# Steps of the cross-attention chain that go on in every cell, and a norm that waits for the queries alone

## The chip, the cores and the metric

The kernel runs on one core of one Trainium2 chip. The metric is the device time of one execution in microseconds; the times of before are those of three runs. The profile is that of one more execution of the same program, with a time of its own.

## What is computed

Two layers work on the same stream of tokens `x`, 2 sequences of 1024 tokens with 256 features, in float32. A context of 64 tokens for each sequence, and a mask over it, come beside it. Both layers have 16 heads of 16 features.

```python
# layer 0
x = x + mha(ln(x), ln(x))                  # self attention, 1024 x 1024 scores per head
x = x + mha(ln_q(x), ln_kv(context))       # cross attention, 1024 x 64 scores per head
h = ln(x); top 2 of 8 experts by h @ router
x = x + sum(gate * (gelu(h @ fc1[e]) @ fc2[e]))
# layer 1
x = x + proj(attention(qkv(ln0(x))))       # self attention
attn = softmax(q(ln1(x)) @ k(context).T * SCALE + (1 - mask) * -10000)
x = x + proj(attn @ v(context))            # cross attention, masked
x = x + fc2(gelu(fc1(ln2(x))))
```

## The kernel before

Tokens lie in tiles of 128; a unit is 512 tokens (four tiles), so that there are four units, two for each sequence. PE's results go to eight PSUM banks that are handed out by `bank()` and given back to the list `free`. PE, DVE, ACT and SP execute in the order in which the program was written down[...].

**The cells of self attention.** `self_attention` (L527) walks through cells (the loop at L960): 64 for each sequence, so 128 cells and two more to finish. A cell is one head, 512 queries and 128 keys in both of two kinds of scores. In each cell stand four score matmuls "b" (L817), whose exponentials ACT takes (L823), and, `LEAD` = 10 cells ahead, four score matmuls "a" (L806), whose maxima DVE takes (L813). In cells 0 to 117 there is something left to look ahead to (`has_a`); `maxima[0]` says so to the rest of the program. Every second cell has the product of exponentials and values (L868) of two cells, whose results ACT copies (L880) and POOL adds up (L881). At the end of a head its maxima are turned into the subtrahend of its queries (`largest`, L714 and L716). The sums of a finished group of heads travel over DRAM (SP: L482, L483, L487, `turns` L499, `by_s` L503), and POOL multiplies by them (L509).

**Everything else is a stream of steps.** All other work is cut into tasks, Python generators that issue some instructions and yield. `Stream` (L132) decides, when the program is built, after which cell a step is issued. A yield above zero is the declared cost of the step, in us of PE; a yield of zero or below declares no cost and asks for a pause, to the next cell or, below zero, for that many us, counted in cells of `CELL` = 2.9 us. `owed` is what the stream may still spend: each cell adds `pace(cell)`, at least the layer's `RATE` (2.5 us in layer 0, 1.1 in layer 1), and it is capped at 3.0 before that. While `owed` exceeds 0.6, `Stream.step` takes a step of the ready task with the earliest last cell, then the highest rank. Steps without cost are also taken only there. In an even cell with `owed` below 2.5 the loop goes straight on to the next cell. What must be there by then is forced with `Stream.until`: `need_heads` (L703) forces the projections that an even head needs in the cell whose look-ahead reaches it. When the loop is over, `Stream.rest` (L179) issues what is left by rank and readiness.

**Tasks.** Keys and queries (`keys` L656, `queries` L665) project a pair of groups of heads and then spread it with eight small DMAs on SP (`spread_head`, L650 to L652, into `KS` and `QS`), in two steps of four without cost. The self attention's output projection of a unit (`project`, L788, its task `go`) has two halves of 2.0 each. Then the chain of cross attention follows for the units in turn (`cross_tasks`, L1077):

- `norm` (mark "cnorm"): the layer norm of four tiles, its turning by PE (L370) and copying by ACT (L377); two steps of 1.0.
- `weigh` (L1104, mark "weighed"): two projections of queries (L1114, 1.72 each), then scores, softmax, turning and products for two groups. If `maxima[0]` holds as it starts, it takes the whole form: scores are copied by ACT (L1159), the mask is added by POOL (L1178), maxima and sums are DVE's (L1168, L1191), the subtraction and division POOL's or DVE's (L1169, L1193), the exponentials ACT's (L1185), and then come the turning (L1201), its copy (L1206) and the product. Otherwise, in layer 1, PE adds the mask with matmuls (L1139), ACT takes exponentials from the turned scores (L1208), and PE makes the sums (L1240, `undivided`) and spreads the reciprocals (L1255, `division`).
- `share` (L1317, mark "cross"): the output projection of cross attention, two halves of 2.0.

In layer 0 `dispatch_task` (L1351) of a unit comes next (norm, router, places of the tokens with their experts; `found` and `rows` follow it) and then the slots of the experts. In layer 1 `forward_norm` (L1844, mark "ready", four roots on POOL: L332 to L335) and `forward_task` (L1852, L1861 and L1873) follow, with 29.8 for each unit.

The order of the chain before: the norm of unit n waits for the mark ("weighed", n - 1), and the whole `weigh` of unit n for its norm and for ("cross", n - 1).

Of the kernel before, what the change touches and what calls it, by code (L numbers as in the profile page):

```python
# [121 lines left out]
class Task:  # L122

    def __init__(self, steps, cost, first=-99, last=None, mark=None, after=(), rank=0):
        self.steps, self.left, self.first = steps, cost, first
        self.soft, self.last = last is None, 9999 if last is None else last
        self.mark, self.after, self.rank = mark, after, rank


class Stream:  # L132
# [20 lines left out]
    def step(self, cell):  # L153
        while True:
            able = [t for t in self.tasks if t.first <= cell and self.made.issuperset(t.after)]
            if not able:
                return None
            cost = self.advance(min(able, key=lambda t: (t.last, -t.rank)), cell)
            if cost and cost > 0.0:
                return cost  # L160

    def pace(self, cell):

# [39 lines left out]
def two_blocks(  # L203
# [228 lines left out]
    def project_task(src, w, first, t0, n):  # L432

        i, p = bank()
        p = p.rearrange("p (c d) -> p c d", d=D)
        for c in range(n):
            for k in range(2):
                nc.tensor.matmul(  # L438
                    p[:, c, :],
                    lhsT=src[:, k, (t0 + c) * P : (t0 + c + 1) * P],  # L440
                    rhs=w[:, W_O + k * D : W_O + (k + 1) * D],
                    start=(k == 0),
                    stop=(k == 1),
                )
        xb = x_sb[:, first : first + n, :]
        nc.vector.tensor_tensor(xb, xb, p[:, :n, :], ALU.add)
        free.append(i)
        yield 2.0
# [78 lines left out]
    def self_attention(layer, tail, heads, arrive, extra, when_ready, beside=None):  # L527
# [5 lines left out]
        w = weights[att]  # L533
# [32 lines left out]
        now = [-99]  # L566
# [221 lines left out]
        def project(b, qh, after=()):  # L788
            def go():
                for t0 in range(0, 4, 2):  # L790
                    yield from project_task(ot[b, qh], w, b * TB + 4 * qh + t0, t0, 2)
                when_ready(b, qh, stream, now[0])

            stream.add(go(), 4.0, last=now[0] + 4, rank=60, after=after)

        def score(kind, cell, j):
            h, n = divmod(cell, 8)
# [162 lines left out]
        for cell in range(ncell + 2):  # L960
            now[0] = cell
            ahead = cell + LEAD
            if ahead < ncell and ahead % 16 == 0:
                need_heads(ahead // 8)
            has_a, has_b = ahead < ncell, cell < ncell
            maxima[0] = has_a
            a = [("a", ahead, j) for j in (2, 3, 0, 1)] if has_a else []
            s = [("b", cell, j) for j in range(4)] if has_b else []
            if has_a:
                slot(s[:2] + a[:2])  # L970
                slot(s[2:] + a[2:])
            elif has_b:
                slot(s)
            if ahead % 8 == 7 and has_a:
                h = ahead // 8
                collect(h)
                stream.add(largest(h), 0.75, first=cell + 1, last=cell + 2, mark=("QB", h))
            if (cell + 1) % 8 == 0 and cell + 1 < ncell:
                stream.until(("QB", (cell + 1) // 8))
            for go in later.pop(cell, []):  # L980
                go()
            owed = min(owed, 3.0) + max(stream.pace(cell), 0.0 if has_a else 2.0)
            if cell >= 2 and cell % 2 == 0:
                product([c for c in (cell - 2, cell - 1) if c not in alone])
                if owed < 2.5:
                    continue
            most = 3.0
            while owed > 0.6 and most > 0.0:
                cost = stream.step(cell)
                if cost is None:  # L990
                    break
                owed -= cost
                most -= cost

            if cell % 2 == 1 and most > 2.0 and cell < ncell:
                alone.add(cell - 1)
                product([cell - 1])
# [79 lines left out]
    def cross_tasks(stream, layer, n, pool, first):  # L1077


        att = 2 * layer + 1  # L1080
        w = weights[att]
        b, t0 = n // 2, 4 * n
        name = f"c{layer}{n}"
        held = {}

        def norm():
            xT = held["xT"] = pool.tile([P, 2, 512], F32, tag="cx", name=f"xT_{name}")
            yield from norm_task(t0, 4, "cq" if layer == 0 else "ln1", xT, name)
            if layer == 0:
                add_bias(t0, 4, bias_out[1])  # L1090

        before = [(m, n - 1) for m in ("cross", "weighed")] if n > 0 else ["context"]
        stream.add(norm(), 2.0, mark=("cnorm", n), after=before[1:], first=first,
            rank=67 if layer == 0 else 40)
        stream.add(
            weigh(layer, b, pool, w, name, held), 17.0,
            mark=("weighed", n), after=[("cnorm", n), before[0]], rank=30,
        )
        stream.add(
            share(w, name, t0, held), 5.0, mark=("cross", n),  # L1100
            after=[("weighed", n)], rank=50,
        )

    def weigh(layer, b, pool, w, name, held):  # L1104

        att = 2 * layer + 1
        kbd, vbd = kbds[layer], vbds[layer]
# [3 lines left out]
        for g in range(2):  # L1111
            i, p = bank()
            for k in range(2):
                nc.tensor.matmul(  # L1114
                    p,
                    lhsT=w[:, X_Q + k * D + g * P : X_Q + k * D + (g + 1) * P],
                    rhs=xT[:, k, :],
                    start=(k == 0),
                    stop=(k == 1),
                )  # L1120
            nc.scalar.activation(
                q[:, g, :], p, AF.Identity, bias=cols[:, C_Q[att] + g : C_Q[att] + g + 1]
            )
            free.append(i)
            yield 1.72
        shape = [P, 4 * 2, SK]
        less, pts, whole_scores = {}, {}, set()

# [188 lines left out]
    def share(w, name, first, held):  # L1317

        if held["division"]:
            yield -2.6  # L1320
            held["division"](1)
            yield 0.55
        yield -1.2
        for t0 in range(0, 4, 2):
            yield from project_task(held["ot"], w, first + t0, t0, 2)


    inside = const.tile([P, E], F32, name="inside")
# [245 lines left out]
    class Mixture:  # L1574
# [3 lines left out]
        def __init__(self, slotw, epool):  # L1578


            self.slotw, self.epool = slotw, epool
            self.caps = []

            self.spare = const.tile([P, W_2], F32, name="spare")


            self.w, self.done, self.ready = ({}, {}), [0, 0], (set(), set())
            self.xs = {}
            self.places, self.ends = [], []
            self.turned = self.nrows = 0  # L1590
            self.end = NEVEN

            self.next = None
# [604 lines left out]
```

## Times and profile before

| | us |
|---|---|
| median of three runs | 1615.26 |
| lowest and highest of them | 1612.68, 1616.85 |
| the profiled execution | 1614.59 |
| its span, from first to last instruction | 1612.8 |
| layer 0, cells 0 to 127 (first L823 of each) | 53.5 to 565.7 |
| layer 1, cells 0 to 127 | 950.9 to 1431.1 |
| layer 1, from the tail's first L1114 to the end | 1439.9 to 1612.8 |

The mean granted TensorE clock is 0.984. A line of groups reads: source line, engine, operation, out and in with shapes, count, then busy us, mean ns of one, and the idle time just before them with what ended it. A line of waits reads: engine and line that waited, what it waited for, us in total, times, the longest. Durations below are of the one profiled execution.

Each layer's cells take about a third of the span. In between lies the end of layer 0 with the experts (to about 900), in which PE has its work from the slots.

### The profile page before, as it was taken

The numbers are of one execution on the slowest core, as the hardware profiler recorded it, in microseconds if no ns is written. First come the engines' busy times: TensorE is split into PE (matmuls) and PEld (weight loads), VectorE is DVE, ScalarE is ACT, GpSimd is POOL, SyncE is SP. The second block draws the span as 40 slices with busy tenths as digits, with TensorE's granted clock in tenths as the row PEclk, the third lists the DMA queues.
The fourth block names the chain that finished last, engine by engine and source line by source line (L and its number), as shares of the span: only waits on it lengthen the run. The fifth ranks groups of instructions, "written<-read, shape, count | busy, mean of one in ns | idle before, by whom it ended". The sixth has DMA issues, their size and how long they took to land. (4 is left out here: it accounts for less than half of the span.)

```text
span 1612.8 us, 27523 instructions
## 1 busy us (share of the span) xinstructions
PE 1560.5 (97%) x10182; PEld 853.7 (53%) x10182; DVE 1013.8 (63%) x2178; ACT 939.3 (58%) x1821; POOL 472.2 (29%) x589
## 2 busy tenths in 40 slices
PE   7999999999999888899999999999999999999998
PEld 3533443443444356688888753344344444446766
DVE  5788776877878856511114458876777878845400
ACT  3488777866867752332333337876777877864321
POOL 2234333433623302311112032411333525511000
PEclk9899999998999999999999999999999999999999
DMA  5236211100100214475656321101110001000000
GB/s 157 113 134 226 81 34 29 34 14 21 41 25 18 67 49 134 153 272 189 203 190 234 92 73 28 35 21 22 34 34 21 22 27 70 22 28 1 14 13 26
DMA packets 55749, 120.98 MB, mean 75 GB/s; under 512 B 12218, under 2 KB 26428, under 8 KB 55228
## 3 DMA queue, kind: packets, MB, share of 16 engines
q1 hardware_dynamic: 51772, 109.02, 21.0%
q0 software_dynamic: 3456, 9.51, 1.6%
q8 instruction: 82, 1.34, 0.3%
q10 hardware_dynamic: 384, 0.66, 0.2%
q14 instruction: 55, 0.45, 0.1%
HBM read 71.64 MB, written 38.88 MB: 69 GB/s over the span
## 5 line engine op out<-in xcount | busy, mean ns | idle before, releaser
L813 DVE TENSOR_REDUCE mx_s<-banks 128x1 f32<-128x512 f32 x1024 | 633.2, 680 | 187.0 <-PE banks L806 182.5
L823 ACT ACTIVATE pt_s<-banks 128x512 f32<-128x512 f32 x1024 | 532.9, 611 | 134.8 <-PE banks L806 107.0
L806 PE MATMUL banks<-KS,QS 16*128 16x512 f32 x2048 | 535.0, 631 | 0.2 <-issue 0.2
L817 PE MATMUL banks<-qb_s,KS 32*128 32x512 f32 x2048 | 516.5, 624 | 7.2 <-DVE qb_s L716 2.3
L881 POOL TENSOR_TENSOR acc_s<-acc_s,part_s 128x512 f32<-128x512 f32 x151 | 191.6, 1269 | 370.3 <-ACT part_s L880 369.2
L817 PEld LDWEIGHTS banks<-qb_s,KS 32*128 32x128 f32 x2048 | 179.3, 187 | 194.5 <-DVE mx_s L813 116.3
L868 PE MATMUL banks<-pt_s,v_s 128*20 128x512 f32 x2048 | 265.8, 604 | 2.6 <-DVE mx_s L813 1.9
L806 PEld LDWEIGHTS banks<-KS,QS 16*128 16x128 f32 x2048 | 199.1, 185 | 64.9 <-issue 29.5
L1731 PE MATMUL banks<-w_slot,h_s 128*128 128x256 f32 x640 | 145.2, 384 | 0.0
L868 PEld LDWEIGHTS banks<-pt_s,v_s 128*20 128x20 f32 x2048 | 42.4, 98 | 191.7 <-ACT pt_s L823 142.9
L1731 PEld LDWEIGHTS banks<-w_slot,h_s 128*128 128x128 f32 x640 | 121.7, 192 | 20.4 <-DVE mx_s L813 1.5
L1740 DVE SCALAR_TENSOR_TENSOR ys<-banks,gate,b 128x256 f32<-128x256 f32 x40 | 19.3, 483 | 172.0 <-PE banks L1731 167.7
L880 ACT COPY part_s<-banks 128x512 f32<-128x512 f32 x166 | 100.3, 605 | 45.8 <-PE banks L868 41.3
L1746 POOL DMA_INDIRECT results<-ys,to x40 | 38.7, 967 | 261.5 <-DVE ys L1740 183.2
L1707 ACT ACTIVATE h_s<-banks,w_slot 128x256 f32<-128x256 f32 x104 | 43.6, 470 | 111.3 <-issue 64.0
L1701 PE MATMUL banks<-xsT,w_slot 128*128 128x256 f32 x416 | 96.2, 383 | 0.9 <-ACT xsT L377 0.9
L1701 PEld LDWEIGHTS banks<-xsT,w_slot 128*128 128x128 f32 x416 | 78.0, 191 | 15.4 <-DVE mx_s L813 2.3
L636 PE MATMUL banks<-xT_s,w_att 128*128 128x512 f32 x128 | 63.9, 635 | 0.5 <-DVE mx_s L813 0.5
L1864 ACT ACTIVATE h_f<-banks,w_ff 128x512 f32<-128x512 f32 x32 | 22.0, 687 | 69.7 <-PE banks L1861 69.7
L1873 PE MATMUL banks<-w_ff,h_f 128*128 128x256 f32 x256 | 57.3, 380 | 0.0
L1707 ACT ACTIVATE h_s<-banks,spare 128x256 f32<-128x256 f32 x56 | 23.5, 470 | 57.3 <-issue 33.4
L1861 PE MATMUL banks<-hT_f,w_ff 128*128 128x512 f32 x128 | 56.8, 594 | 0.0
(282 smaller groups left out, 1666.0 us busy)
## 6 DMA issues: line engine op xcount, KB each, us to landing
w_slot<-in_ff_w_dram SPq DMA_DIRECT2D x40, 576.0 KB
sorted_rows<-fill SPq DMA_DIRECT2D x36, 520.0 KB
w_slot<-in_ff_w_dram SPq DMA_DIRECT2D x26, 514.0 KB
whole<-acc_s SPq DMA_DIRECT2D x30, 256.0 KB
spare<-in_ff_w_dram SPq DMA_DIRECT2D x14, 514.0 KB
xs<-sorted_rows SPq DMA_DIRECT2D x20, 260.0 KB
y<-results SPq DMA_DIRECT2D x16, 256.0 KB
QS<-stq_s SPq DMA_DIRECT2D x124, 32.0 KB
```

What stands on the lines that cost most here:

```text
L636: nc.tensor.matmul(p, lhsT=w[:, at + k * D + pair * P : at + k * D + (pair + 1) * P], rhs=xT[b][:, k, blk * 512 : (blk + 1) * 512], start= ...
L806: nc.tensor.matmul(sc, lhsT=QS[h % 4][r, qc * P : (qc + 1) * P], rhs=K[r, kh * 512 : (kh + 1) * 512], start=True, stop=True,)
L813: return i, lambda: nc.vector.tensor_reduce(mx[h][:, qc, j, kh : kh + 1], sc, AX.X, ALU.max)
L817: nc.tensor.matmul(sc, lhsT=K[r, n * P : (n + 1) * P], rhs=QB[h][r, :], start=True, stop=True)
L823: nc.scalar.activation(pt, sc, AF.Exp, scale=SCALE)
L868: nc.tensor.matmul(o[32 * j : 32 * j + VW, :], lhsT=V[b][:, cell % 8, 4 * g + j, :], rhs=exps.pop((cell, j)), start=(cell == cells[0]), st ...
L880: nc.scalar.copy(part, o)
L881: helper().tensor_tensor(acc[h], acc[h], part, ALU.add)
L1701: nc.tensor.matmul(ph[:, n, :], lhsT=w[:, at : at + P], rhs=xT[:, k, :], start=(k == 0), stop=(k == 1),)
L1707: nc.scalar.activation(h1[:, f, :], ph[:, n, :], AF.Gelu, bias=w[:, W_B1 + f : W_B1 + f + 1])
L1731: nc.tensor.matmul(py, lhsT=h1[:, f, h * P : (h + 1) * P], rhs=w[:, f * D : (f + 1) * D], start=(f == 0), stop=(f == 7),)
L1873: nc.tensor.matmul(py[:, n, :], lhsT=h1[:, f, t * P : (t + 1) * P], rhs=w2[:, f * D : (f + 1) * D], start=(f == 0), stop=(f == 7),)
```

## The change

A task can be `steady`. The output projection `go`, and the norm, `weigh` and `share` of the cross-attention chain, are made so. In each cell with something to look ahead to, `Stream.go_on` takes every step of the ready steady tasks, until they pause or end, whatever `owed` says; what they cost is taken off `owed` and off the cell's limit `most`. A yield of 0.0 is put between the halves of the two projections. `weigh` sets a mark ("asked", n) once its query projections are issued, and the norm of unit n + 1 waits for that mark in place of ("weighed", n). `weigh` itself still waits for its norm and for the `share` before it.

```diff
--- before.py
+++ after.py
@@ -123,8 +123,10 @@
 
 
 
-    def __init__(self, steps, cost, first=-99, last=None, mark=None, after=(), rank=0):
-        self.steps, self.left, self.first = steps, cost, first
+    def __init__(
+        self, steps, cost, first=-99, last=None, mark=None, after=(), rank=0, steady=False
+    ):
+        self.steps, self.left, self.first, self.steady = steps, cost, first, steady
         self.soft, self.last = last is None, 9999 if last is None else last
         self.mark, self.after, self.rank = mark, after, rank
 
@@ -158,6 +160,15 @@
             cost = self.advance(min(able, key=lambda t: (t.last, -t.rank)), cell)
             if cost and cost > 0.0:
                 return cost
+
+    def go_on(self, cell):
+
+
+        total = 0.0
+        for t in [t for t in self.tasks if t.steady]:
+            while t in self.tasks and t.first <= cell and self.made.issuperset(t.after):
+                total += max(0.0, self.advance(t, cell) or 0.0)
+        return total
 
     def pace(self, cell):
 
@@ -789,9 +800,11 @@
             def go():
                 for t0 in range(0, 4, 2):
                     yield from project_task(ot[b, qh], w, b * TB + 4 * qh + t0, t0, 2)
+                    if t0 == 0:
+                        yield 0.0
                 when_ready(b, qh, stream, now[0])
 
-            stream.add(go(), 4.0, last=now[0] + 4, rank=60, after=after)
+            stream.add(go(), 4.0, last=now[0] + 4, rank=60, after=after, steady=True)
 
         def score(kind, cell, j):
             h, n = divmod(cell, 8)
@@ -983,8 +996,13 @@
             if cell >= 2 and cell % 2 == 0:
                 product([c for c in (cell - 2, cell - 1) if c not in alone])
                 if owed < 2.5:
+                    if has_a:
+                        owed -= stream.go_on(cell)
                     continue
             most = 3.0
+            going = stream.go_on(cell) if has_a else 0.0
+            owed -= going
+            most -= going
             while owed > 0.6 and most > 0.0:
                 cost = stream.step(cell)
                 if cost is None:
@@ -1089,19 +1107,22 @@
             if layer == 0:
                 add_bias(t0, 4, bias_out[1])
 
-        before = [(m, n - 1) for m in ("cross", "weighed")] if n > 0 else ["context"]
-        stream.add(norm(), 2.0, mark=("cnorm", n), after=before[1:], first=first,
-            rank=67 if layer == 0 else 40)
+        before = ("cross", n - 1) if n > 0 else "context"
         stream.add(
-            weigh(layer, b, pool, w, name, held), 17.0,
-            mark=("weighed", n), after=[("cnorm", n), before[0]], rank=30,
+            norm(), 2.0, mark=("cnorm", n), after=[("asked", n - 1)] if n > 0 else [], first=first,
+            rank=67 if layer == 0 else 40, steady=True,
+        )
+        stream.add(
+            weigh(layer, b, pool, w, name, held, lambda: stream.made.add(("asked", n))), 17.0,
+            mark=("weighed", n), after=[("cnorm", n), before], rank=30,
+            steady=True,
         )
         stream.add(
             share(w, name, t0, held), 5.0, mark=("cross", n),
-            after=[("weighed", n)], rank=50,
+            after=[("weighed", n)], rank=50, steady=True,
         )
 
-    def weigh(layer, b, pool, w, name, held):
+    def weigh(layer, b, pool, w, name, held, asked):
 
         att = 2 * layer + 1
         kbd, vbd = kbds[layer], vbds[layer]
@@ -1123,6 +1144,7 @@
             )
             free.append(i)
             yield 1.72
+        asked()
         shape = [P, 4 * 2, SK]
         less, pts, whole_scores = {}, {}, set()
 
@@ -1323,6 +1345,8 @@
         yield -1.2
         for t0 in range(0, 4, 2):
             yield from project_task(held["ot"], w, first + t0, t0, 2)
+            if t0 == 0:
+                yield 0.0
 
 
     inside = const.tile([P, E], F32, name="inside")
```

As the program is built, PE has 5489 matmuls in place of 5545.

## The prediction

> **What bounds the kernel now.** I read the page's busy times and slices first, then PE's waits, then the busy time of each engine in stretches cut at the starts of cells, and last the queue of SP around cells 45 to 54 of layer 1.
>
> ```profile
> PE 1560.5 (97%) x10182; PEld 853.7 (53%) x10182; DVE 1013.8 (63%) x2178; ACT 939.3 (58%) x1821; POOL 472.2 (29%) x589
> PE   7999999999999888899999999999999999999998
> PEclk9899999998999999999999999999999999999999
> ```
>
> PE is busy in 97% of the span, in every slice from the second to the last but one; no other engine is near. Only some 52 us (1612.8 - 1560.5) are PE idle, and they are what a better order can win, beside work that is really left out. The longest of PE's waits:
>
> ```profile
> PE banks L370 <- DVE xn_s L358: 9.1, 3, 7.5
> PE banks L370 <- DVE xd_m L1364: 6.5, 1, 6.5
> PE banks L370 <- DVE xn_c L358: 4.9, 3, 1.9
> PE banks L370 <- DMA ctx<-in_ctx_dram: 2.2, 1, 2.2
> PE banks L370 <- DVE xn_f L358: 2.0, 1, 2.0
> ```
>
> Columns: total us, times, longest. All are turns (L370) that wait for a norm; the change can touch the last four. The stretches of layer 1 (cell 104 starts at 1349.7, cell 118 at 1404.4, the tail at 1439.9; columns: length, then busy us and instructions of PE, PEld, DVE, ACT, POOL; then clock, DMA share, GB/s):
>
> ```profile
> 1349.70:1404.40 54.70, 54.04 (x416) 22.39 (x412) 47.92 (x90) 44.61 (x88) 31.72 (x40) 1.00 0.07 21
> 1404.40:1439.90 35.50, 31.72 (x216) 12.03 (x209) 18.48 (x55) 28.65 (x57) 7.90 (x17) 0.99 0.05 16
> 1439.90:1612.80 172.90, 167.44 (x990) 117.04 (x988) 53.10 (x107) 52.45 (x79) 13.09 (x34) 0.99 0.05 16
> ```
>
> PE is full in the cells and in the tail alike, so a step that goes from the tail into the cells is paid there; DVE is at 88% in cells 104 to 117 and ACT at 81% in the next stretch, so added work meets two more engines there. Words of the skill: "matmul busy % (`TensorMatrix` occupancy) is not a good measure of how close you are to roofline" (the Trainium skill, Perfetto Trace Analysis, Identifying the Most-Contended Engine). The trace agrees: 2048 matmuls of L806 at 631 ns would be 1292 us, but its union is 535.0. I therefore price moved work by what cells really took, not by matmul durations.
>
> **What the skill says besides.** The Trainium skill, TensorE: Matmul & The Clock Gate, Part 1: the clock is halved after an idle window of about 3.4 us and restored after a busy one. The trace agrees: the granted clock falls to one half in pieces of 3.4, 6.8, 10.2 and 13.7 us (at 1439.4, 531.4, 391.5, 53.5); half of each is lost. The Trainium skill, DMA: Bandwidth & Descriptors, Issuing engines are not separate DMA queues: the time a sequencer takes to start a DMA "is usually small relative to the DMA itself". Here it isn't for a series: eight issues of one K projection take 4.99 us of SP, 0.62 each.
>
> **The change part by part.** Which cell a step lands in is decided when the program is built, so it can be written out from it. Costs called declared are the kernel's own (Q projection 1.72 twice, scores 1.0, or 1.9 with mask matmuls, and so on).
>
> *Work left out.* In layer 1, `weigh` of unit 2 now begins in cell 111, while `maxima[0]` holds, so it takes the whole form. 16 mask, 32 sum and 8 division matmuls go.
>
> ```profile
> L1139 PE MATMUL banks<-mask_i,ones 1*128 1x128 f32 x128 | 12.9, 282 | 0.0
> L1240 PE MATMUL banks<-pt_c,picks 128*32 128x128 f32 x192 | 8.3, 280 | 3.1 <-issue 3.1
> L1255 PE MATMUL banks<-inv_c,picks 128*128 128x128 f32 x48 | 6.3, 275 | 0.0
> ```
>
> The trace shows each matmul of the program as two, so 32 of 128, 64 of 192 and 16 of 48 go. By busy time and idle: 12.9/4 = 3.2, (8.3 + 3.1)/3 = 3.8, 6.3/3 = 2.1: at most 9.1. But much of it runs beside other matmuls: in the timeline a masked score step is 0.87 us longer than one without, `undivided` 0.98 longer than a product, a division 0.9. Two of each: 5.5, which I take. The declared costs drop by 5.8: four score steps by 0.9, two `undivided` and two divisions by 0.55; two of the score steps come after cell 117, keep their mask and no longer declare it (1.8).
>
> *Layer 1, tail.* Declared work after the cells goes from 175.9 to 157.7: 16.7 of unit 2's `weigh`, 0.55 of its `share`, 1.0 of `ready(1)`. The tail took 172.9 for 175.9, so 0.98 each gives -17.9. The half clock at 1439.4 lay on waits that go: 3.4/2, of which 1.4 on work: -1.4.
>
> *Layer 1, cells to 103.* In come the rest of unit 1's `weigh` (13.14 declared for 5.44: +7.7) and its `share` (+4.0), out goes one output projection step (-2.0): +9.7. Price: over 58 pairs of cells, from the start of the first exponentials (L823) of one pair to the next, a straight line through time against declared cost gives 6.3 us a pair plus 0.83 per declared us; each step that declares nothing but works on ACT, POOL or DVE costs about 0.2. 9.7 x 0.83 + 9 x 0.2 = +9.9. Bounds: 7 (they fill PE's own gaps) and 12 (at 1.0 each plus such steps).
>
> *Layer 1, cells 104 to 117.* Out: 4.85 of unit 1's `weigh`. In: 5.44 of unit 2's, `cnorm` 2 with 2.0, an output projection step 2.0: +4.6, at 0.83 +3.8. DVE gets some 3.7 us more (two norms of 5.3 us each, by L358, L344 and L345 there, for sums and maxima of some 7) on 47.9 of 54.7: no longer time for it, but little slack. Bounds +1 and +7. Both `ready` norms' roots run on POOL together at cell 109, 28 small operations of 0.2 to 0.7 us; the turn that needs them stands two cells later: nothing, 1 if late.
>
> *Layer 1, cell 118 to the tail.* -1.85 declared, which the two undeclared masks make up, and the waits of 1.3 and 2.0 us at 1436 and 1439 go (`cnorm` 2 and `ready(1)` are done long before). But ACT gets some 4 copies of turned weights, 3 exponentials and 2 more copies, 0.6 us each: 28.65 + 5 = 34 in a stretch that PE could run in 31. ACT decides, with its own gaps: +0.7, bounds -3.3 and +4.
>
> *The queue of SP.* This is the cost that I did not expect from the diff. `go_on` takes its cost off `owed`, and 4.44 go in cell 48 of layer 1, so `owed` is below 0.6 for several cells. The steps of `keys` and `queries` of head 8 that issue their DMAs declare nothing, but are taken only while `owed` exceeds 0.6. Before, they stood in cells 45 to 50:
>
> ```profile
> 1121.88 4.99 SPq L652 DMA_DIRECT2D KS<-stk_s  x8
> 1126.96 2.43 SPq L652 DMA_DIRECT2D QS<-stq_s  x4
> ...
> 1139.68 2.45 SPq L652 DMA_DIRECT2D QS<-stq_s  x4
> 1143.89 0.33 SPq L499 DMA_DIRECT2D turns<-sums_s  x1
> 1145.32 0.65 SPq L503 DMA_DIRECT2D by_s<-turns  x1
> ```
>
> Now `need_heads(8)` forces all sixteen at cell 54, just ahead of the scores that read KS[4] and QS[0], and on SP behind `turns` and `by_s`, which keep their place. From the start of cell 51 (1141.0): `by_s` is issued at 5.0 (1145.97), eight KS take 5.0, four QS 2.4, landing about 1.6 (SP's own wait for `whole<-acc_s` in this stretch): 14.0. PE comes to those scores after three cells of 3.3: 9.9. PE stands still for 4.1, with everything behind it in its order. Such an idle time has cost half a clock before; I add 3.4, half of a 6.8 us piece. +7.5; bounds 3.5 (no half clock) and 11.
>
> *Layer 0.* No unit changes its form. The tail loses a 1.15 step and the wait for xd_m (6.5) gets two more slot steps ahead of it (-3.7), the context's DMA and `cnorm` 3 are reached earlier and wait longer (+1.2, +1.5), and part of a half clock at 630 to 657 goes (-1.4): -3.5. Its cells get that step and DVE work of `found` 2: +1.5. Together -2.0, bounds -6 and +3.
>
> *Waits and yields.* The norm of unit n waits for ("asked", n - 1), less than before. `xT` and `q` have their own buffers in turn, so PE waits for no reader that is not done. The added `yield 0.0` puts the second half of an output projection into the next cell; no instruction is added by it, and 2.0 in a cell instead of 4.0 is within what cells took before.
>
> **Sum.** Layer 1: -17.9 - 1.4 + 9.9 + 3.8 + 0.7 + 7.5 = +2.6. Layer 0: -2.0. Together +0.6 on the profiled execution's 1614.6 (span 1612.8 and 1.8 around it): 1615.2. The median of the runs lies 0.7 above it: 1615.9.
>
> **Rivals.** *The gain stays.* PE's work falls by 5.5 and its waits by 3, and the sixteen DMAs land in time because PE reaches cell 54 later than I think (its cells are longer by some us by then). Then +0.6 - 7.5 = -6.9: 1608.4. For it: PE is full everywhere, so less work should be less time. Against it: the SP arithmetic misses by 4 us, more than the cells' spread. *Slower: the cells pay full price.* The steps come in lumps (4.44 in one cell) between the scores that feed ACT and DVE; what these lose they can't make up where they are at 88% and 81%. Moved work then costs 1.0 instead of 0.83 on 14.3 declared (+2.4), and the stretch after cell 118 is ACT's at +4 (+3.3): 1615.9 + 5.7 = 1621.6. It decides once cells and stall together take over 24 us, the 21 that leave tail and layer 0 plus the 3 that the waits give. For it: DVE and ACT in the fences above. Against it: the straight line held for cells with up to 4 us declared. *That nothing changes* can't be: instructions differ in number.
>
> **Chances.** Forecast, within the 0.3% (4.8 us) that a measurement can tell from no change: 0.38. Faster, 1608.4: 0.26. Slower, 1621.6, or more with a half clock twice: 0.36, since the unknown terms (stall, ACT) reach further up than down. The range goes to 1605.5, where the faster case with layer 0's better bound leaves 1 in 10, and to 1627, the slower one with the stall's upper bound and a little more.
>
> **What would show it.** Right: the tail from L1114 is about 155 us; the first L806 of cell 54 in layer 1 waits some 4 us for a DMA of QS or KS, the clock falls there; L1139 counts 96, L1240 128, L1255 32; the waits for `xn_c` and `xn_f` at the end of the cells are gone; cells 36 to 103 of layer 1 are 10 us longer, stall apart. Wrong: PE doesn't wait in cell 54, or waits of DVE or ACT for over 3 us stand elsewhere in the cells.

## The result and the profile after

The changed kernel takes 1643.91 us (median of 4 runs, 1640.23 to 1644.87), the kernel before beside it 1616.05 (1612.68 to 1617.32). The ratio is 1.0175, with an interval from 1.0154 to 1.0195: slower by some 28 us. The profiled executions differ by 25.7 us in their spans. The page's head, as shown of before:

```profile
span 1638.5 us, 27336 instructions
PE 1582.3 (97%) x10070; PEld 855.1 (52%) x10070; DVE 1019.4 (62%) x2176; ACT 943.1 (58%) x1832; POOL 489.5 (30%) x618
PE   7999999999999988899999999999899999999998
PEclk9899999999999899999999999999999999999999
```

PE has 112 matmul records fewer, as predicted, and is nevertheless 22 us longer "busy". The share is 97% as before, so this view doesn't show the loss at all. A table by stages does. Each boundary is the start of the first exponentials of a cell (L823 before, L836 after: the change moves later lines by 11 to 24):

| stage | before | after | difference | forecast |
|---|---|---|---|---|
| up to cell 36 of layer 0 | 180.8 | 178.7 | -2.1 | |
| layer 0, cells 36 to 127 | 384.8 | 408.8 | **+24.0** | +1.5 |
| to layer 1's cell 0 | 385.2 | 384.9 | -0.3 | -3.5 |
| layer 1, cells 0 to 44 | 163.8 | 164.3 | +0.5 | |
| cells 44 to 60 | 63.6 | 78.6 | +15.0 | +17.4 for cells to 104 |
| cells 60 to 104 | 171.4 | 178.7 | +7.3 | (with the line above) |
| cells 104 to 118 | 54.7 | 58.5 | +3.8 | +3.8 |
| cells 118 to 127 | 26.7 | 29.5 | +2.8 | -18.6 to the end |
| to the end | 181.7 | 156.3 | -25.4 | (with the line above) |

Layer 1 as a whole comes out at +4.1, where +2.6 was forecast. Layer 0 has nearly the whole loss, in its cells, where the same work is declared before and after.

PE's waits, the same view as before, with the columns total us, times, longest:

```profile
PE banks L381 <- DVE xn_s L369: 8.7, 3, 7.1
PE banks L830 <- DVE mx_s L826: 4.6, 8, 1.9
PE banks L381 <- DVE xd_m L1388: 4.2, 1, 4.2
PE banks L381 <- DMA ctx<-in_ctx_dram: 4.2, 1, 4.2
PE banks L819 <- DMA QS<-stq_s: 4.1, 1, 4.1
PE banks L381 <- DVE xn_c L369: 2.7, 1, 2.7
```

The wait for xd_m fell from 6.5 to 4.2 (-2.3, where the prediction had -3.7) and that for xn_f is gone, as foreseen. New is L819, a score matmul that waits for a DMA. Layer 1's stretches that were shown of before, cell 104 to 118, to the tail, and the tail (PE starts the tail's chain before the last copy, so the boundary at 1488 is rough):

```profile
1394.10:1452.70 58.60, 57.15 (x404) 24.00 (x397) 49.72 (x100) 43.70 (x85) 32.92 (x63) 1.00 0.06 20
1452.70:1488.00 35.30, 34.85 (x283) 14.57 (x282) 23.87 (x42) 32.79 (x66) 3.53 (x3) 1.00 0.03 9
1488.00:1638.50 150.50, 145.29 (x733) 100.22 (x731) 40.19 (x87) 40.07 (x62) 11.00 (x32) 1.00 0.06 20
```

ACT is at 93% in the second, where it was at 81%: the stretch didn't shrink, though PE's waits in it went. The tail is shorter by more than 20.

### The profile page after: what moved, and what is told of

Same layout as the page of the kernel before. It is cut to its first block, busy times and chain, and to the rows that moved or that the text cites. A ratio compares the mean times of both kernels' runs of the same rounds, so it can differ in the third digit from the quotient of the medians.

```text
span 1638.5 us, 27336 instructions
## 1 busy us (share of the span) xinstructions
PE 1582.3 (97%) x10070; PEld 855.1 (52%) x10070; DVE 1019.4 (62%) x2176; ACT 943.1 (58%) x1832; POOL 489.5 (30%) x618
## 3 DMA queue, kind: packets, MB, share of 16 engines
q1 hardware_dynamic: 51772, 109.02, 20.5%
## 5 line engine op out<-in xcount | busy, mean ns | idle before, releaser
L836 ACT ACTIVATE pt_s<-banks 128x512 f32<-128x512 f32 x1024 | 534.4, 612 | 150.3 <-PE banks L819 112.4
L819 PE MATMUL banks<-KS,QS 16*128 16x512 f32 x2048 | 549.7, 635 | 6.2 <-DMA QS<-stq_s 4.1
L830 PE MATMUL banks<-qb_s,KS 32*128 32x512 f32 x2048 | 524.0, 625 | 10.2 <-DVE mx_s L826 4.6
L894 POOL TENSOR_TENSOR acc_s<-acc_s,part_s 128x512 f32<-128x512 f32 x154 | 195.6, 1270 | 351.5 <-ACT part_s L893 348.7
L830 PEld LDWEIGHTS banks<-qb_s,KS 32*128 32x128 f32 x2048 | 183.7, 187 | 195.7 <-DVE mx_s L826 114.4
L881 PE MATMUL banks<-pt_s,v_s 128*20 128x512 f32 x2048 | 272.9, 617 | 0.6 <-ACT pt_s L836 0.5
L819 PEld LDWEIGHTS banks<-KS,QS 16*128 16x128 f32 x2048 | 201.8, 186 | 80.0 <-issue 34.2
L1191 POOL TENSOR_TENSOR sc_c<-sc_c,mx_c 128x512 f32<-128x512 f32 x40 | 41.8, 1044 | 58.4 <-DVE mx_c L1190 56.5
```

What stands on the lines that cost most here:

```text
L819: nc.tensor.matmul(sc, lhsT=QS[h % 4][r, qc * P : (qc + 1) * P], rhs=K[r, kh * 512 : (kh + 1) * 512], start=True, stop=True,)
L830: nc.tensor.matmul(sc, lhsT=K[r, n * P : (n + 1) * P], rhs=QB[h][r, :], start=True, stop=True)
L836: nc.scalar.activation(pt, sc, AF.Exp, scale=SCALE)
L881: nc.tensor.matmul(o[32 * j : 32 * j + VW, :], lhsT=V[b][:, cell % 8, 4 * g + j, :], rhs=exps.pop((cell, j)), start=(cell == cells[0]), st ...
L894: helper().tensor_tensor(acc[h], acc[h], part, ALU.add)
```

## What happened in cell 54 of layer 1

First SP's queue, then PE, in the timeline of the changed kernel:

```profile
1173.21 0.32 SPq L510 DMA_DIRECT2D turns<-sums_s  x1
1174.63 0.61 SPq L514 DMA_DIRECT2D by_s<-turns  x1
1175.29 5.12 SPq L663 DMA_DIRECT2D KS<-stk_s  x8
1180.50 4.95 SPq L663 DMA_DIRECT2D QS<-stq_s  x8
```

```profile
1178.62 1.13 PE L830 MATMUL banks<-qb_s,KS 32*128 32x512 f32 x4
1183.79 2.84 PE L819 MATMUL banks<-KS,QS 16*128 16x512 f32 x7 [4.05 <-DMA QS<-stq_s]
```

All sixteen DMAs of head 8 stand behind `by_s`, and PE stands still for 4.05 us; 4.1 was the forecast. Before, they were spread from 1121.88 to 1142.1. The clock is halved for 10.2 us behind it, so 5.1 are lost, where I took 3.4. That step holds by its mechanism and nearly by its size.

## What happened in layer 0

Cells 76 to 83 take 36.3 us before (from 350.2) and 45.4 after (from 354.3). The second line of each view is the stretch of cells 104 to 127. Before:

```profile
350.20:386.50 36.30, 35.61 (x250) 14.72 (x250) 27.58 (x56) 26.96 (x51) 13.47 (x26) 1.00 0.05 16
475.10:565.70 90.60, 85.94 (x630) 34.81 (x622) 77.12 (x177) 70.15 (x139) 32.17 (x52) 0.96 0.12 39
```

After:

```profile
354.30:399.70 45.40, 43.00 (x269) 17.17 (x265) 32.00 (x69) 27.56 (x55) 14.17 (x16) 0.89 0.04 13
482.70:587.60 104.90, 99.07 (x635) 37.49 (x629) 78.85 (x175) 72.48 (x142) 34.16 (x42) 0.90 0.10 34
```

The column after POOL is the granted clock: 0.89 and 0.90 where it was 1.00 and 0.96. In the record of the clock, the pieces at one half in these cells add up to 17.0 us before (10.2 at 391.5, 6.8 at 531.4) and to 30.6 after (3.4 at 365.8, 6.8 at 376.1, 6.8 at 519.4, 10.2 at 546.7, 3.4 at 570.6). Half of the difference, 6.8, is lost to the clock. The rest of the 24 is time at full clock. One level deeper, the pieces around cell 78:

```profile
350.00:365.80 15.80, 14.68 (x98) 5.84 (x94) 12.05 (x25) 11.92 (x23) 6.86 (x18) 1.00 0.01 2
365.80:369.20 3.40, 3.40 (x15) 1.27 (x14) 3.30 (x9) 0.59 (x1) 0.33 (x1) 0.51 0.00 0
369.20:376.10 6.90, 5.03 (x37) 2.75 (x39) 6.73 (x17) 4.73 (x10) 2.50 (x2) 0.99 0.00 1
376.10:382.90 6.80, 6.80 (x26) 1.59 (x23) 2.92 (x7) 2.01 (x4) 0.59 (x1) 0.50 0.00 0
```

In the second and third line DVE is busy for 3.30 of 3.40 and 6.73 of 6.90 us: it looks like the bound there, and not PE. In the fourth, on the half clock, a product of 16 matmuls takes 3.62 us, and behind it begins the lump of cell 80, two query projections and the first scores. Until the first of these scores comes, DVE has nothing to do for 8.34 us:

```profile
381.40 4.43 PE L1135 MATMUL banks<-xT_c,w_att 128*128 128x512 f32 x8
387.56 0.69 DVE L1190 TENSOR_REDUCE mx_c<-sc_c 128x8 f32<-128x512 f32 x1 [8.34 <-ACT sc_c L1181]
```

So DVE is first the bound and then starved, and its share of the whole stretch is lower than before (32.00 of 45.40 us, where it was 27.58 of 36.30). DVE's operations in the third piece, by its timeline:

```profile
369.17 0.73 DVE L369 TENSOR_SCALAR xn_c<-x_sb,mv_c,rs_c 128x256 f32<-128x256 f32 x2
369.82 0.69 DVE L727 TENSOR_TENSOR qb_s<-QS,banks 128x512 f32<-128x512 f32 x1
370.43 0.87 DVE L1432 SCALAR_TENSOR_TENSOR lg_m<-hot_m,lg_m 128x32 f32<-128x32 f32 x1
371.22 1.28 DVE L1433 TENSOR_SCALAR xd_m<-first_m 128x4 f32<-128x4 f32 x1
...
373.40 2.48 DVE L826 TENSOR_REDUCE mx_s<-banks 128x1 f32<-128x512 f32 x4
```

The norm of unit 1's chain (xn_c), the subtrahend of a head (qb_s) and the choice of experts of `dispatch` 0 (L1424 to L1433, small, but one after the other) stand in one row; no maximum is taken from 369.2 to 373.4, so no bank of the scores ahead comes back to PE. L1432 and L1433 are also slow here: 0.87 and 1.28 us, where the median of each is 0.19 and 0.17. Both run beside an operation of POOL, and L1433 ends with it:

```profile
371.20 1.27 POOL L894 TENSOR_TENSOR acc_s<-acc_s,part_s 128x512 f32<-128x512 f32 x1
```

Before, the choice of experts came five cells later, and unit 1's norm in the same cells as here. Cells 84 to 87, where that choice stood, take 16.9 us now and 21.1 before, so cells 76 to 87 together are 4.8 us longer, and not 9.1.

That is what the trace suggests. The experiments had to show whether it is the cause, since the lump is as good a suspect.

## The experiments

All ratios are to the kernel before, run beside on the same chip; before itself had medians from 1609 to 1617 on these chips, so times of different runs are compared by their ratios only, and stages by the profiled executions, one for each kernel. "Layer 0's cells" are its cells 36 to 127: 384.8 us before, 408.8 changed. Two kernels below leave layer 0 exactly as before, and their profiles have 387.4 and 384.8 there, so a difference under some 3 us between two profiles says little.

### Which layer, which part

**heads_fed.** DMA steps of keys and queries are taken in each cell.

```diff
-        for t in [t for t in self.tasks if t.steady]:
+        for t in [t for t in self.tasks if t.steady or (t.left < 0.2 and t.mark[0] in ("K", "Q"))]:
```

> The changed kernel, but the steps of keys and queries that only issue DMAs are taken in each cell too, whatever owed says. Starved queue (my theory for layer 1): the wait of 4.05 us for QS at cell 54 of layer 1 goes and with it the half clock behind it (10.2 us, 5.1 lost): 1643.9 - 9.2, so 1634 to 1636. Rival, the wait is hidden by DVE, which is behind anyway: the wait goes, but the time falls by less than 3: 1641 or more.

1.0134 (1.0108 to 1.0161), 6.6 us less than the change's 1.0175. The wait for QS and the half clock behind it are gone; cells 44 to 60 of layer 1 take 70.8 instead of 78.6 (-7.8, where 9.2 was expected). The wait was real, and not hidden by DVE.

**go_on_layer1** and **go_on_layer0.** `go_on` in one layer alone.

```diff
-            going = stream.go_on(cell) if has_a else 0.0
+            going = stream.go_on(cell) if has_a and layer == 1 else 0.0
```

(and likewise in the even cells; `layer == 0` in the other).

> go_on in layer 1 alone; layer 0 keeps the split yields and the norm that waits for the queries, its order is nearly that of before. If the 24 us that layer 0's cells grew come from taking steps whatever the supply, they go: 1643.9 - 24 = 1620, and layer 1 keeps its +4 to +6. Rival: layer 0's loss comes from half clocks that fall by chance of where waits lie (7 us of the 24) and from the split halves: then only some of it goes, 1630 or more.

> go_on in layer 0 alone; layer 1 has the split yields and the earlier norm by supply. Layer 0 keeps its +24: 1616 + 24 = 1640, less what the earlier norm gains in layer 1 (waits of 3.3 us at the end of the cells): 1636 to 1641. If layer 0's loss is chance, below 1630.

1.0043 (1.002 to 1.0066) and 1.0131 (1.0105 to 1.0156). Layer 0's cells are at 387.7 and 409.4. So three quarters of the loss come from `go_on` in layer 0.

**asked_only.** The norm that waits for the queries and the split halves, `go_on` nowhere.

```diff
-            going = stream.go_on(cell) if has_a else 0.0
+            going = 0.0
```

> The norm that waits for the queries alone and the split halves, no go_on anywhere. Declared work in cells and tails is the same as before (255.2 and 316.9), the lumps of 4.0 are gone, unit 2 of layer 1 starts in cell 119 and so keeps its masks. Theory of lumps (work taken together in a cell costs more than spread): 3 waits of 3.3 us go and eight lumps of 4.0 are halved: 1610 to 1614. Rival, only the sum of work and waits counts: 1613 to 1616.

1.001 (0.9998 to 1.0023): no difference. Both expectations missed by a few us; the waits at the end of layer 1's cells went (its last stage is 160.3 instead of 181.7), but its cells 44 to 127 take 336.7 instead of 316.4 (some 15 us more declared there and a half clock of 10.2 us). The expectation had the declared work of cells and tail as before; in the program as built some 20 us of it moved from layer 1's tail into its cells. With `go_on` in place the earlier mark does nothing: the planner then makes the same order of steps with the old mark, since each norm is added to the stream only after the unit before it is done.

### Lumps: the theory that fell

In an even cell `go_on` takes two query projections and the first scores together, 4.44 declared. My first theory was that such lumps starve ACT and DVE.

**q_apart.** A pause after each query projection.

```diff
             yield 1.72
+            yield 0.0
         asked()
```

> The changed kernel with a yield of 0.0 after each of weigh's two query projections, so that they and the first score step (4.44 declared) come in three cells instead of one; everything else goes on whatever the supply. Lumps (what is taken together stalls the feeding of ACT and DVE, about 2 us for each of six such cells, and half clocks follow): 1643.9 - 12 and a half clock less, 1628 to 1633. Rival for layer 0, the chain's steps crowd with the norm of the dispatch on DVE (cells 76 to 88 and 108 to 119): 1639 or more.

1.0153 (1.0128 to 1.0178): hardly less than changed, as the rival's total had it, for layer 1 got new waits in turn (PE waits 2.9 us for the maxima of a head in cell 86 and 2.5 at a norm's turning in cell 110). But layer 0's cells went from 408.8 to 395.3, 13.5 less. That seemed to support lumps. However, the chain now ended two cells later, and the dispatch behind it moved with it, from cells 68 and 100 to 70 and 102.

**one_step.** `go_on` ends after one step with a cost.

```diff
                 total += max(0.0, self.advance(t, cell) or 0.0)
+                if total > 0.0:
+                    return total
```

> The changed kernel, but go_on ends after the first step with a cost in each cell. Keys and queries of head 8 are then spread in cells 43 to 50 (no starvation), and no lump is left that go_on makes. Lumps and starvation as the causes: 1643.9 - 9 (layer 1's queue) - 6 (layer 1's lumps) - 12 or more of layer 0's 24: 1613 to 1618. Rival, what costs is going beyond the supply at all: 1628 or more.

1.0046 (1.0029 to 1.0064), some 21 us less than changed, between the two ranges expected; layer 0's cells at 387.7. This version still goes on beyond the supply, so that alone isn't the cost. It can't tell lumps from the dispatch either: that starts in cell 72 here.

**no_even.** No `go_on` in even cells with little owed.

```diff
-                    if has_a:
-                        owed -= stream.go_on(cell)
                     continue
```

> The changed kernel without go_on in the even cells that have their product and little owed. The lumps stay (cells 49, 80 and 112 in layer 0, 52, 84 and 115 in layer 1), though fewer of them beside a product. If it is the cell with its product that can't take more: 1622 or less. If lumps count wherever they are: it loses the starvation of head 8 alone, 1632 to 1636.

1.0106 (1.0082 to 1.013). Layer 0's cells take 410.7: no gain there, though a lump moved out of its product's cell (48 to 49) and the dispatch began in 69. Layer 1 lost its starvation. The cell with a product is no special place. The second expectation, 16 to 20 us over a before of 1616, is met with 17.

**before_lump.** The opposite test: the kernel before, with the lump put in.

```diff
             free.append(i)
-            yield 1.72
+            if not maxima[0]:
+                yield 1.72
+        lump = 3.44 if maxima[0] else 0.0
...
-                us = sum(costs.get(step, 0.0) for step, *_ in now)
+                us = sum(costs.get(step, 0.0) for step, *_ in now) + lump
+                lump = 0.0
```

> The kernel before, with one edit: in the whole form, weigh's two query projections and its first score step are one step (4.44) instead of three. They come in cells 51, 80 and 112 of layer 0 and 55 and 97 of layer 1; the rest of the order is within a cell of before. Lumps: 2 us each and a half clock for some, 8 to 15 us slower than before. Rival (crowding on DVE, or work that goes beyond its supply elsewhere): within 3 us of before.

1.0007 (0.9996 to 1.0017). Five lumps, in cells 51, 80 (there with a step of the dispatch, 6.4 in all) and 112 of layer 0 and 55 and 97 of layer 1, cost nothing that can be measured; layer 0's cells take 387.3 instead of 384.8. The test is smaller than it looks: in four of these cells the kernel before already takes both projections together (3.44), so the edit adds 1.0 there and 2.72 in cell 80. But then the change's lumps are hardly larger than those of before. By themselves lumps are not the cause, and the theory fell.

### The place of the dispatch

**dispatch_late.** Changed, with the dispatch of unit 0 six cells later.

```diff
+        if unit == 0:
+            yield -17.4
         mv, rs = yield from statistics(src, 4, name)
```

> The changed kernel; the dispatch of unit 0 in layer 0 waits six cells, so that its norm, router and places come in cells 74 to 93 as before the change and not beside the norm of unit 1 (73 to 79). Crowding on DVE: cells 76 to 83 of layer 0, 9 us longer than before the change, lose 5 or more: 1643.9 - 5 or more, on a chip with before at 1616. Lumps: under 3 us less.

1.018 (1.0162 to 1.0198): nothing gained. Cells 36 to 80 take 6.4 us less (190.3 for 196.6), as crowding says, though 3.4 declared us left them with the dispatch; but cells 80 to 104 take 10.6 more (117.9 for 107.4), with one half clock of 20.5 us at 403.6. The profiled execution is the slowest of six (1647.19, the median is 1639.67), so these stages are on the long side. The dispatch stands beside unit 1's softmax steps here, but so it does in the kernel before, where cells 36 to 104 take 294.2 and not 308.2. Its old cells alone don't bring the old time back, and the expectation for the total was wrong.

**dispatch_2.** Two cells later for units 0 and 1, the lumps left in.

```diff
+        if unit < 2:
+            yield -5.8
         mv, rs = yield from statistics(src, 4, name)
```

> The changed kernel; the dispatches of units 0 and 1 wait two cells more (70 and 102 instead of 68 and 100, where q_apart has them), the lumps of 4.44 stay. If the dispatch's place was what q_apart changed: cells 36 to 127 of layer 0 near 395, as there (409 as changed). If the lumps were: 405 or more.

1.011 (1.0075 to 1.0145). Layer 0's cells take 398.8, 10.0 less than changed. So 10.0 of the 13.5 that q_apart gained can be had by moving the dispatch alone. The 10.0 are mostly unit 0's: cells 36 to 80 take 190.4 for 196.6 with the same declared work. Cells 104 to 127 take 101.2 for 104.8, though unit 1's dispatch starts in cell 102 there, as before the change, when they took 90.6.

**before_dispatch_out** and **after_dispatch_out.** In both kernels the dispatches of units 0 and 1 come after the cells. All is still computed.

```diff
-                    mark=("dispatch", n),
+                    first=130 if n < 2 else -99, mark=("dispatch", n),
```

> The kernel before, with the dispatches of units 0 and 1 of layer 0 taken after the cells (first=130); all is still computed. It is the base for the next run: layer 0's cells 36 to 127, 384.8 us before, should lose about 8 declared us and their DVE work, so 370 to 378, with fewer half clocks; the work after the cells grows by 8 or more.

> The changed kernel with the same edit; the chain keeps its cells. Crowding with the dispatch: cells 36 to 127 of layer 0 are within 6 us of the run beside it, where the two kernels differ by 24 with the dispatches in. Rival, the chain's own places (steps beside products, turns that come sooner) cost it: still 15 us or more longer.

1.0164 (1.0133 to 1.0195) and 1.0284 (1.0249 to 1.032): both dearer, since the dispatch is then on the path after the cells (436 to 438 us for 385 there, half clocks of 61 and 65 us among them). What counts is the stretch of cells. The first expectation missed there: 361.0 us is 23.8 less than with the dispatches in, for 8.3 declared us. First the kernel before, then the changed one, both without dispatches, cells 76 to 83 and 104 to 127:

```profile
350.20:382.00 31.80, 31.46 (x241) 14.46 (x234) 24.59 (x42) 24.76 (x49) 11.51 (x13) 1.00 0.06 18
462.10:541.80 79.70, 78.71 (x608) 31.68 (x600) 61.10 (x108) 67.95 (x133) 23.27 (x31) 1.00 0.05 15
```

```profile
352.00:385.70 33.70, 33.63 (x250) 14.51 (x250) 25.30 (x44) 26.71 (x51) 14.68 (x19) 1.00 0.05 17
465.20:548.40 83.20, 81.98 (x613) 32.32 (x606) 60.86 (x110) 69.06 (x136) 26.78 (x34) 1.00 0.04 14
```

The clock is 1.00 in all four, and the 9.1 and 14.3 us between the kernels have become 1.9 and 3.5. Layer 0's cells together take 361.0 and 369.4: a difference of 8.4 where it was 24.0. So 15.6 us of the loss need the dispatches in the cells together with the moved chain; where in the cells they must stand, this pair doesn't tell. The 8.4 that stay are over the 6 of crowding and under the 15 of the rival.

**apart_dispatch_out.** after_dispatch_out with q_apart's pauses, executed once.

> The changed kernel with the dispatches of units 0 and 1 after the cells, and a yield of 0.0 after each of weigh's query projections. If the lumps of 4.44 make the 8.5 us that layer 0's cells 36 to 127 still differ by: 361 to 364. If lumps cost nothing, as in the kernel before with lumps put in: 367 to 371.

Layer 0's cells take 367.5, the upper case: taking the lumps apart is worth 1.9 of the 8.4, less than two profiles can differ by.

### Is there a gain under the costs?

**one_step_layer1_fed.** `go_on` in layer 1 alone, one costing step in a cell, DMA steps fed: the edits above together.

> go_on in layer 1 alone, with one costing step in a cell, and the DMA steps of keys and queries taken whatever owed says. Layer 1 then has the whole form for unit 2 (5.5 us of PE left out) and the waits at its end gone, without lumps and without the stalled queue. If the gain of the change is real under its costs: 1616 - 5 to - 9, 1607 to 1611. Rival, work in the cells is dearer than in the tail wherever it is put: 1615 to 1619.

1.0039 (1.0024 to 1.0055), no gain, and over the rival's range too. Layer 1's cells 44 to 127 take 330.9 instead of 316.4, and its last stage gives back only 8.8 of these 14.5 (172.9 instead of 181.7): PE waits 4.5 us for ot_s and 1.8 for xn_f there, and the clock is at one half for 10.2 us.

**layer1_fed.** Layer 0 exactly as before (no split, no earlier mark, no `go_on`), layer 1 changed and fed. **layer1_fed_apart** has q_apart's pauses as well.

> Layer 0 exactly as before; layer 1 as changed, with the DMA steps of keys and queries taken whatever owed says. By stages of the run with both layers changed: layer 1's cells and tail give 659 against 662 before: 2 to 4 us faster than before. If the stages don't add up so, same as before or slower.

> The same, with the two query projections and the first scores in three cells. Lumps in layer 1 (cells 48, 80, 112) at 1 to 2 us each: another 3 to 6 us less, so 5 to 9 us faster than before. Rival, lumps cost only in layer 0, where the supply is higher: the same as layer1_fed within 2 us.

0.9977 (0.9968 to 0.9986) and 1.0058 (1.0037 to 1.0078). layer1_fed is faster than both kernels, by 3.7 us on 1609.45 (2.3 to 5.2 by the interval): the gain exists in layer 1, as small as its stages said. Taking the lumps apart there makes it worse, which neither expectation had. Cells 60 to 118 take 250.1 instead of 237.3, with half clocks that cost 12 of these 13, behind waits of PE for a norm (2.4) and for the maxima of a head (1.5): steps that came two cells later stand in worse places. Lumps don't cost what I thought in layer 1 either.

## Why the prediction was wrong

**Held.** The order of units; the matmuls left out (L1161, L1262 and L1277 have 96, 128 and 32 records as foretold); the starved steps of head 8 and the 4.05 us of PE in cell 54; the waits of 3.3 us at the end of layer 1's cells. Cells 104 to 118 cost 3.8 for 3.8. From cell 118 to the end layer 1 has -22.6 where the sum had -18.6 (-17.9 - 1.4 + 0.7). Cells 0 to 104 have +22.8 for +17.4: the half clock in cell 54 took 5.1 instead of 3.4, and moved work cost more than 0.83 for each declared us. How much more, heads_fed and layer1_fed show, which have neither the stall nor a half clock there: cells 0 to 104 still take some 15 us more than before, for 9.7 declared us that were priced at +9.9. Layer 1 in all: +4.1 for +2.6. That it came so close is luck in part, since the cells cost 5.4 more than forecast and the end gave 4.0 more.

**Failed: the step for layer 0.** It said that no unit changes its form, that its cells get one step and a little DVE work, "+1.5", and in all "-2.0, bounds -6 and +3". The measured cells are +24.0. I priced what moves by declared PE time, as a straight line over all pairs, and in layer 0 the declared time in the cells hardly changes. What it left out, and so put at nothing, is what the moved chain and the dispatch do to each other on the engines they share. The dispatch follows the `share` of its unit, so it came six cells earlier for unit 0 (68 for 74) and two for unit 1 (100 for 102), while the norms of units 1 and 2 stayed at cells 73 and 105. The trace of before had the warning: DVE is at 85% in cells 104 to 127 (77.12 of 90.60), and half clocks stood at 391.5 and 531.4, both in a dispatch. With the dispatches taken out of the cells, the kernel before lost 23.8 us there for 8.3 declared. The prediction looked at DVE only in layer 1.

The 24.0 us, by the runs:

- 15.6 need the dispatches in the cells. Of these 6.8 is what the clock record shows as lost. The other 8.8 is time at full clock; that it is PE waiting for banks which DVE still has to read, and which the page counts as busy, is read from the pieces around cell 78 and not measured for the whole.
- How much of the 15.6 is the dispatch's place is known in part: 10.0 go when both dispatches start two cells later (dispatch_2). But the old cells don't restore the old time, in dispatch_late for unit 0 and in dispatch_2 for unit 1, so the chain's own new order beside the dispatch counts as well. Which part of that order it is stays open.
- 1.9 are perhaps the lumps (one execution).
- About 6.5 stay open, 4.5 of them in cells 36 to 80. asked_only has the split halves and 184.4 there, so they aren't it. More declared work isn't it either: cells 36 to 126 have 100.88 declared us before and after. What remains is that the chain's steps stand in other cells beside products and projections of heads; this was not taken apart.

The 15.6 is shown as an effect of both being in the cells together; that it goes by way of DVE is read from the trace. A kernel in which the choice of experts runs on another engine was not tried.

**The rivals.** "The cells pay full price", with 1621.6, had the right side, and in layer 1 its 1.0 for each declared us was nearer to what was paid than 0.83, though still too low. But before_lump and layer1_fed_apart speak against its mechanism (lumps between the scores), and the loss in layer 0 was not in it. "The gain stays" was right for layer 1 with the queue mended: 4.9 of its 6.9 us were layer 1's, and layer1_fed has 3.7.

## What to carry to other kernels

Where two chains of small steps share one in-order engine, moving one of them forward is to be priced by what it meets there, cell by cell and on each engine, and not by its own cost: list the engine's busy share at the new place, the other chain's steps included, over stretches as short as a cell or two, since here a bound engine and a starved one average out within four cells. A planner that takes its allowance for one kind of work starves the free steps of the others, DMA issues above all, and these then land just where they are needed. And a busy share of 97% says nothing on such a loss; stages, the granted clock and the waits do.

## What was unexpected in the hardware

The granted clock fell to one half at 365.8 although no wait of PE longer than 0.6 us is shown in the 15 us ahead (0.58 and 0.53 us; PE busy 14.68 of 15.80). The Trainium skill (TensorE: Matmul & The Clock Gate, Part 1) tells of an idle window of about 3.4 us. The pieces here have that length or multiples of it, but no such idle time came ahead. Nor did it ahead of the one at 391.5 in the kernel before (the longest wait there is 1.39 us), so that the agreement which the prediction found was in the lengths alone. My reading, not tested by itself, is that it is enough for PE to have little to do for a while because DVE holds its banks. It isn't the whole rule: in the 3.4 us ahead of 365.8 PE is busy for 2.87 us and DVE for 3.30, and in those from 352.1 to 355.5 for 2.90 and 3.31, where no half clock followed. The cost of SP's series agreed with before: 16 issues in 10.2 us (1175.29 to 1185.45), 0.63 each.

Small operations of DVE took several times longer beside POOL. In layer 0's cells 36 to 127, each DVE operation that took over 0.25 us more than the median of its kind and shape overlaps an operation of POOL: 13 of them before and 14 changed, 13.3 and 15.0 us over their medians in all. Without the dispatches there are three in each kernel, with 3.0 and 3.1 us. So a part of what the dispatch costs in the cells is DVE's time beside POOL, in both kernels nearly alike; no run tests it by itself.
